# One-hot products for 36 groups of layer 1 and 20 of layer 0 in a two-layer GNN kernel

## The chip, the cores and the metric

The kernel runs on one core of one Trainium2 chip. The metric is the device time of one execution in microseconds. TensorE is called PE, VectorE DVE, ScalarE ACT, GpSimd POOL and SyncE SP.

## The reference

There are 12,500 nodes with 48 features and 200,000 edges, sorted by destination. Each layer reads, for every edge, the row of its source node, makes a message, and adds the messages up by destination.

```python
def _L0_gnn_ref(x, edge_index, edge_attr, W1, b1, W2, b2):
    src, dst = (edge_index[0], edge_index[1])
    tmp = jnp.concatenate([x[dst], x[src], edge_attr], axis=1)   # 48 + 48 + 32
    h = jax.nn.relu(tmp @ W1 + b1)                               # hidden 128
    msg = h @ W2 + b2                                            # 48
    return jax.ops.segment_sum(msg, dst, num_segments=N_NODES)

def _L1_gnn_ref(node_feat, edge_feat, src, dst, eps):
    m = jax.nn.relu(node_feat[src] + edge_feat)
    neigh = jax.ops.segment_sum(m, dst, num_segments=N_NODES)
    return (1.0 + eps[0]) * node_feat + neigh

x = _layernorm(x + _L0_gnn_ref(x, edge_index, edge_attr_32, W1, b1, W2, b2))
x = _layernorm(x + _L1_gnn_ref(x, edge_attr_48, src, dst, eps))
```

## The kernel before

The edges are padded to 391 groups of 512 (128 partitions x 4, `NCHUNK` = 391, `TPC` = 4). The nodes are 98 blocks of 128 (`NT` = 98), in 14 segments of 7 blocks (`NSEG`, `NB`). The two layers follow each other, since layer 1 gathers rows that layer 0's last segment writes.

The rows of the source nodes come by `gather` (L201): four indirect DMAs a group, issued by POOL, 128 rows each, from `x` in layer 0 (into the tile `cat`) and from `x1_dram` in layer 1 (into `xs`). The pool `cats` has ten buffers, so POOL can be ahead of the rest. SP loads the edge features for five groups at a time and, in layer 0, a window of projected destination rows (`wcat`) for every group.

The order on each engine is written out by hand. `run` (L443) goes over steps k; in each step it calls every stage for the group that is due, then `lead`. All engines work through their instructions in this order, so a stage's instructions stand behind those of the stages called ahead of it.

- Layer 0, step k: `fetch0` (gathers, five groups ahead), `fill0` (edge features and the one-hot of the destination, two ahead), `sum0` (group k-3: four matmuls of messages with the one-hots on L323, then a DVE addition into `agg` on L318), `message0` (k-2: matmuls on L432, bias on DVE), `hidden0` (k-1: matmul on L424, relu on ACT), `turn0` (k: four transposes on L417, copied by DVE to `cat_t`), then `lead0`, which loads and projects the next segment (`project`, 14 times: transposes L267, matmuls L272, with ACT copies between) at set steps.
- When the last group of a segment is summed, `finish0` transposes the sums, does residual and layer norm, writes `x1_dram`, and splits the result into three bfloat16 pieces that add up to it, in `xp` (128 x 98 blocks x 3 x 48, in SBUF).
- Layer 1, step k: `fetch1`, `fill1`, `sum1` (group k-1, matmuls and addition into `agg`), `message1` (k: DVE addition on L495, relu on ACT), then `lead1`.

For 28 of layer 1's groups (every 13th from 26) POOL gathers nothing. Their rows are made by products. `products` takes two such groups at a time. `place` turns their source indices into a tile `which` in PSUM that holds, for every edge, block + 1 at the row that the node has in its block, and zero elsewhere (DVE L515, PE transposes L520). For each of the 98 blocks `select` (L525) makes a one-hot of 128 x 1024 on DVE, and `multiply` (L530) does eight matmuls of 128 x 144 with the block's pieces in `xp`, added up in PSUM. At the end `edge_of` closes the sums, and three DVE reductions (L570) add the pieces up. The generator is advanced once a step, four blocks at a time (`BPS`). A batch of two groups takes 25 steps and one more for the end. PE multiplies in one step what DVE selected in the step before.

PSUM has eight banks. The sums of the products share the tiles `ph`, `pm` and `pt` with layer 0 (`pt` has two buffers), and `px` serves the projections and the ends of segments.

Of the kernel before, what the change touches and what calls it, by code (L numbers as in the profile page):

```python
# [58 lines left out]
FIRST = 26  # L59
EVERY = 13  # L60
NPE = 28
BATCH = 2
PIECES = 3
BPS = 4

PE_GROUPS = [FIRST + EVERY * i for i in range(NPE)]
assert PE_GROUPS[-1] < NCHUNK and NPE % BATCH == 0

# [60 lines left out]
def windowed(ctx, tc, dram, flag, x, src, dst, e32, e48, w1, b1, w2, b2, eps, out):  # L129
    nc = tc.nc  # L130
    const = ctx.enter_context(tc.tile_pool(name="const", bufs=1))
    onehots = ctx.enter_context(tc.tile_pool(name="onehots", bufs=2 * BPS))
# [90 lines left out]
    pb = psum.tile([P, NCHUNK], F32, name="px")  # L223
# [6 lines left out]
    def check_windows():  # L230
        flat = rel.rearrange("p g t -> p (g t)")
        most = node.tile([P, 1], F32, name="most")
        nc.vector.tensor_reduce(most, flat, AX.X, ALU.max)
        least = node.tile([P, 1], F32, name="least")
        nc.vector.tensor_reduce(least, flat, AX.X, ALU.min)
        over = node.tile([P, 1], F32, name="over")
        nc.vector.tensor_scalar(over, most, float(W), None, op0=ALU.is_ge)
        bad = node.tile([P, 1], F32, name="bad")
        nc.vector.scalar_tensor_tensor(bad, least, 0.0, over, op0=ALU.is_lt, op1=ALU.add)
        pf = psum.tile([1, 1], F32, name="px")  # L240
        nc.tensor.matmul(pf, bad, ones[:P, 0:1], start=True, stop=True)
        nc.vector.tensor_copy(flag, pf)


    part = const.tile([P, NPE, TPC], F32, name="part")
    block = const.tile([P, NPE, TPC], F32, name="block")

    def split_src():
        first = FIRST * TPC
        some = src_i[:, first : first + (NPE - 1) * EVERY * TPC].rearrange(  # L250
            "p (i c) -> p i c", c=EVERY * TPC
        )[:, :, 0:TPC]
        last = src_i[:, PE_GROUPS[-1] * TPC : (PE_GROUPS[-1] + 1) * TPC]
        bits = node.tile([P, NPE, TPC], I32, name="bits")
        for op, by, plus, to in (
            (ALU.bitwise_and, Q - 1, 0.0, part), (ALU.logical_shift_right, 7, 1.0, block)
        ):
            nc.vector.tensor_scalar(bits[:, : NPE - 1, :], some, by, None, op0=op)
            nc.vector.tensor_scalar(bits[:, NPE - 1, :], last, by, None, op0=op)
            nc.vector.tensor_scalar(to, bits, plus, None, op0=ALU.add)  # L260


    def project(s):
        for b, n in ((s * NB, 4), (s * NB + 4, 3)):
            pt = psum.tile([D, n, Q], F32, name="px")
            for k in range(n):
                nc.tensor.transpose(pt[:, k, :], x_seg[s][:, b + k - s * NB, :], ident)  # L267
            xt = node.tile([D, n, Q], F32, name="xt")
            nc.scalar.activation(xt, pt, AF.Copy)
            pa = psum.tile([Q, n, HID], F32, name="px")  # L270
            for k in range(n):
                nc.tensor.matmul(pa[:, k, :], xt[:, k, :], w1a, start=True, stop=True)  # L272
            a = node.tile([Q, n, HID], F32, name="a")
            nc.scalar.activation(a, pa, AF.Copy)
            row = b * Q - seg_start(s)
            nc.scalar.dma_start(
                a_dram[s][row : row + n * Q, :].rearrange("(t p) d -> p t d", p=Q), a
            )
            if b == s * NB and s > 0:
                row = b * Q - seg_start(s - 1)  # L280
                nc.scalar.dma_start(a_dram[s - 1][row : row + TAIL, :], a[0:TAIL, 0, :])
            if b > s * NB and s + 1 < NSEG:
                nc.scalar.dma_start(a_dram[s + 1][0:HEAD, :], a[Q - HEAD : Q, n - 1, :])
# [43 lines left out]
    def segment_sums(layer, s):  # L327
# [7 lines left out]
        pn = psum.tile([Q, NB, D], F32, name="px")  # L335
# [26 lines left out]
    def finish0(s):  # L362
# [6 lines left out]
        for i in range(PIECES):  # L369
            piece = xp[:, s * NB : (s + 1) * NB, i, :]  # L370
            nc.scalar.activation(piece, x1, AF.Copy)
            if i < PIECES - 1:
                rest = node.tile([Q, NB, D], F32, name="rest")
                nc.vector.tensor_tensor(rest, x1, piece, op=ALU.subtract)
                x1 = rest
# [20 lines left out]

    cat, ph, h, pm, hot = {}, {}, {}, {}, {}

    def fetch0(g):
        cat[g] = cats.tile([P, TPC, Q], F32, name="cat")  # L400
        for j in range(TPC):
            gather(cat[g][:, j, W : W + D], x, g, j)

    def fill0(g):
        e = load_edges("e32c", e32, DE, g)
        nc.scalar.activation(cat[g][:, :, W + D :], e, AF.Copy)
        one_hot(cat[g][:, :, :W], g)
# [6 lines left out]
    def turn0(g):  # L414
        pt = psum.tile([Q, TPC, P], F32, name="pt", bufs=2)
# [27 lines left out]
    def run(stages, finish, lead):  # L443
# [3 lines left out]
        for k in range(first, NCHUNK + last):  # L447
            for f, d in stages:
                g = k - d
                if 0 <= g < NCHUNK:  # L450
                    f(g)
                    if d == last:
                        for s in finishes.get(g, []):
                            finish(s)
            lead(k)

    def lead0(k):
# [7 lines left out]
        if k == 16:  # L465
            split_src()

    for g in range(AHEAD):
# [5 lines left out]
        finish0, lead0,  # L474
# [3 lines left out]
    made = {}  # L478

    def fetch1(g):  # L480
        if g in PE_GROUPS:
# [10 lines left out]
    def message1(g):  # L492
        m = work.tile([P, TPC, D], F32, name="m")
        xs = made.pop(g) if g in PE_GROUPS else cat.pop(g)
# [5 lines left out]
    def sum1(g):  # L500
        pa = reduce_tiles(hot.pop(g), h.pop(g))
        add_window(1, g, pa)


    tiles = BATCH * TPC
    PER = 512 // (PIECES * D)
    SUMS = ("ph", "pm", "pt")

    def place(first):

        which = psum.tile([Q, tiles, P], BF16, name="pt", bufs=2)
        for i in range(BATCH):
            which_e = work.tile([P, TPC, Q], BF16, name="which_e")
            for j in range(TPC):
                nc.vector.tensor_scalar(  # L515
                    which_e[:, j, :], iota_q, part[:, first + i, j : j + 1],
                    block[:, first + i, j : j + 1], op0=ALU.is_equal, op1=ALU.mult,
                )
            for j in range(TPC):
                nc.tensor.transpose(which[:, i * TPC + j, :], which_e[:, j, :], ident16)  # L520
        return which

    def select(which, b):
        o = onehots.tile([Q, tiles, P], BF16, name="o")
        nc.vector.tensor_scalar(o, which, float(b + 1), None, op0=ALU.is_equal)  # L525
        return o

    def multiply(ps, o, b):
        for k in range(tiles):
            nc.tensor.matmul(  # L530
                ps[k // PER][:, k % PER, :], o[:, k, :], xp[:, b, :, :],
                start=False, stop=False, skip_group_check=True,
            )

    def edge_of(ps, start):
        for t in ps:
            n = t.shape[1] * PIECES * D
            nc.tensor.matmul(
                t.rearrange("p k c d -> p (k c d)"), zeros[:, :P], zeros[:, :n],
                start=start, stop=not start,  # L540
            )

    zeros = const.tile([1, 512], BF16, name="zeros")
    nc.vector.memset(zeros, 0.0)

    def products():

        for first in range(0, NPE, BATCH):
            due = PE_GROUPS[first]
            which = place(first)  # L550
            ps = [
                psum.tile([P, min(PER, tiles - k * PER), PIECES, D], F32, name=name,
                          bufs=2 if name == "pt" else 1)
                for k, name in enumerate(SUMS)
            ]
            edge_of(ps, True)
            last = []
            for b in range(0, NT, BPS):
                now = [(b + i, select(which, b + i)) for i in range(min(BPS, NT - b))]
                for c, o in last:  # L560
                    multiply(ps, o, c)
                last = now
                yield due
            for c, o in last:
                multiply(ps, o, c)
            edge_of(ps, False)
            xs = work.tile([P, tiles, D], F32, name="made")
            for k, t in enumerate(ps):
                n = t.shape[1]
                nc.vector.tensor_reduce(  # L570
                    xs[:, k * PER : k * PER + n, :], t.rearrange("p k c d -> p k d c"),
                    AX.X, ALU.add,
                )
            for i in range(BATCH):
                made[PE_GROUPS[first + i]] = xs[:, i * TPC : (i + 1) * TPC, :]
            yield due

    work1 = products()

    def lead1(k):  # L580
        next(work1, None)
# [4 lines left out]
    run([(fetch1, -AHEAD), (fill1, -2), (sum1, 1), (message1, 0)], finish1, lead1)  # L586
# [211 lines left out]
```

## Time and profile before

| | |
|---|---|
| time, median of 10 runs | 3839.95 us (3836.3 to 3842.09) |
| the profiled execution | 3840.98 us, span 3839.2 us |
| mean granted PE clock | 0.786 of full |
| POOL, gathers of layer 0 | 1564, mean 949 ns, 1484.7 us busy |
| POOL, gathers of layer 1 | 1452, mean 962 ns, 1397.2 us busy |
| PE busy | 2849.9 us (74% of the span) |
| DVE busy | 1893.8 us (49%) |
| ACT busy | 564.0 us (15%) |

In a group's line the profile gives line, engine, operation, the tile written and those read, and the count; then busy time and mean duration of one; then the engine's idle time just before, with what ended it. In a timeline's line stand the start and the length in us, and in brackets the idle time ahead of it. The ends of matmuls are modelled, so starts are safer to compare than lengths. The line numbers are those of the kernel before.

### The profile page before, as it was taken

How to read it: one execution, taken by the hardware profiler on the slowest of the kernel's cores; microseconds unless marked ns; L12 is line 12 of the kernel's file. 1: busy time of each engine (PE TensorE's matmuls, PEld its weight loads, DVE VectorE, ACT ScalarE, POOL GpSimd, SP SyncE). 2: the span in 40 equal slices, each digit the busy share in tenths (PEclk: the TensorE clock that was granted, in tenths of full speed). 3: DMA queues.
4: the chain of work that ended last, by engine and by line, in shares of the span. 5: the costliest groups of instructions: out<-in, count | busy, mean ns of one | idle time of the engine just before them, and what ended most of it. 6: DMA issues, size and time to landing. Idle time of an engine off the chain costs nothing. (4 is left out here: it accounts for less than half of the span.)

```text
span 3839.2 us, 67581 instructions
## 1 busy us (share of the span) xinstructions
PE 2849.9 (74%) x23396; PEld 2202.8 (57%) x23396; DVE 1893.8 (49%) x4618; ACT 564.0 (15%) x1329; POOL 2883.8 (75%) x3025
## 2 busy tenths in 40 slices
PE   7888888888888888888876666667677676767631
PEld 4555555556555555556555666656666565656631
DVE  3333333333333333333356776767677677767731
ACT  2222212212212212212210000000000000000000
POOL 7777777777777777777767777777777777777776
PEclk8787777787777877877788888878877888888765
DMA  3222222222222222222222221222222222212221
GB/s 71 43 45 48 43 45 46 48 40 48 48 39 45 49 41 47 49 38 46 41 44 39 50 43 33 55 45 43 38 50 43 45 43 50 43 32 55 45 43 28
DMA packets 293005, 171.68 MB, mean 45 GB/s; under 512 B 109664, under 2 KB 292400, under 8 KB 292656
## 3 DMA queue, kind: packets, MB, share of 16 engines
q0 software_dynamic: 96512, 74.31, 14.4%
q1 hardware_dynamic: 179248, 84.31, 8.1%
q10 hardware_dynamic: 16896, 8.69, 0.8%
q8 instruction: 185, 3.03, 0.3%
q14 instruction: 164, 1.34, 0.1%
HBM read 154.45 MB, written 12.62 MB: 44 GB/s over the span
## 5 line engine op out<-in xcount | busy, mean ns | idle before, releaser
L201 POOL DMA_INDIRECT cat<-in_x_dram,src_i x1564 | 1484.7, 949 | 481.3 <-issue 343.5
L201 POOL DMA_INDIRECT xs<-x_dram,src_i x1452 | 1397.2, 962 | 458.4 <-issue 341.1
L530 PEld LDWEIGHTS <-o 128*128 128x128 bf16 x10976 | 849.1, 112 | 23.6 <-DVE o L525 1.0
L525 DVE TENSOR_SCALAR o<-pt 128x1024 bf16<-128x1024 bf16 x1372 | 848.6, 677 | 5.4 <-PE pt L520 5.4
L419 DVE COPY cat_t<-pt 128x512 f32<-128x512 f32 x391 | 270.1, 691 | 899.9 <-PE pt L417 899.9
L323 PE MATMUL pa<-hot,msg 128*48 128x48 f32 x3128 | 257.8, 235 | 557.4 <-ACT msg L497 557.1
L417 PEld LDWEIGHTS pt<-ident,cat 128*128 128x128 f32 x1564 | 264.1, 175 | 634.4 <-DMA cat<-in_x_dram,src_i 369.3
L424 PE MATMUL ph<-cat_t,wcat 128*128 128x512 f32 x782 | 573.7, 824 | 0.8 <-DVE cat_t L419 0.8
L323 PEld LDWEIGHTS pa<-hot,msg 128*48 128x48 f32 x3128 | 204.8, 145 | 640.9 <-ACT msg L497 620.9
L417 PE MATMUL pt<-ident,cat 128*128 128x128 f32 x1564 | 390.1, 348 | 242.7 <-DMA cat<-in_x_dram,src_i 238.7
L530 PE MATMUL ph<-xp,o 128*128 128x144 bf16 x4116 | 565.8, 255 | 0.2 <-DVE o L525 0.2
L530 PE MATMUL pm<-xp,o 128*128 128x144 bf16 x4116 | 563.8, 254 | 0.0
L432 PE MATMUL pm<-w_sb,h 128*128 128x48 f32 x3128 | 533.5, 324 | 1.3 <-ACT h L426 1.3
L432 PEld LDWEIGHTS pm<-w_sb,h 128*128 128x128 f32 x3128 | 480.0, 235 | 28.1 <-ACT h L426 2.3
L426 ACT ACTIVATE h<-ph,b_sb 128x512 f32<-128x512 f32 x391 | 268.4, 686 | 1363.4 <-PE ph L424 1345.5
L530 PE MATMUL pt<-xp,o 128*128 128x144 bf16 x2744 | 455.2, 254 | 0.0
L495 DVE TENSOR_TENSOR m<-xs,e48c 128x192 f32<-128x192 f32 x363 | 130.8, 360 | 541.4 <-DMA xs<-x_dram,src_i 540.4
L497 ACT ACTIVATE msg<-m 128x192 f32<-128x192 f32 x391 | 141.8, 363 | 1608.6 <-DVE m L495 1604.8
L323 PE MATMUL pa<-cat,msg 128*48 128x48 f32 x3128 | 263.0, 239 | 33.7 <-DVE msg L434 30.9
L323 PEld LDWEIGHTS pa<-cat,msg 128*48 128x48 f32 x3128 | 209.9, 148 | 113.0 <-issue 53.3
L434 DVE TENSOR_TENSOR msg<-pm,b_sb 128x192 f32<-128x192 f32 x391 | 139.3, 356 | 231.3 <-PE pm L432 230.6
L318 DVE TENSOR_TENSOR agg<-agg,pa 48x48 f32 x782 | 150.6, 193 | 175.3 <-PE pa L323 124.3
(79 smaller groups left out, 1063.5 us busy)
## 6 DMA issues: line engine op xcount, KB each, us to landing
e48c<-in_e_dram SPq DMA_DIRECT2D x78, 480.0 KB
cat<-in_x_dram,src_i POOLq DMA_INDIRECT x1564
e32c<-in_e_dram SPq DMA_DIRECT2D x78, 320.0 KB
xs<-x_dram,src_i POOLq DMA_INDIRECT x1452
wcat<-a SPq DMA_DIRECT2D x391, 24.0 KB
a<-a ACTq DMA_DIRECT2D x14, 256.0 KB
a<-a ACTq DMA_DIRECT2D x14, 192.0 KB
x_seg<-in_x_dram SPq DMA_DIRECT2D x14, 168.0 KB
```

The costliest lines, as they stand in the source:

```text
L201: nc.gpsimd.indirect_dma_start(out=t, out_offset=None, in_=table, in_offset=bass.IndirectOffsetOnAxis(ap=src_i[:, g * TPC + j : g * TPC + ...
L318: nc.vector.tensor_tensor(cols, cols, pa, op=ALU.add)
L323: nc.tensor.matmul(pa, msg[:, j, :], hot[:, j, :], start=j == 0, stop=j == TPC - 1)
L417: nc.tensor.transpose(pt[:, j, :], cat[g][:, j, :], ident[:P, :P])
L419: nc.vector.tensor_copy(cat_t, pt)
L424: nc.tensor.matmul(ph, wcats[g % NW], h[g], start=True, stop=True)
L426: nc.scalar.activation(t, ph, AF.Relu, bias=b1_sb)
L432: nc.tensor.matmul(pm[:, j, :], h[g][:, j, :], w2_sb, start=True, stop=True)
L434: nc.vector.tensor_tensor(msg, pm, b2_sb[:, None, :].to_broadcast([P, TPC, D]), op=ALU.add)
L497: nc.scalar.activation(msg, m, AF.Relu)
L525: nc.vector.tensor_scalar(o, which, float(b + 1), None, op0=ALU.is_equal)
L530: nc.tensor.matmul(ps[k // PER][:, k % PER, :], o[:, k, :], xp[:, b, :, :], start=False, stop=False, skip_group_check=True,)
```

## The change

- The groups by product are now given by `BY_PRODUCT`: ten pairs in layer 0 (first 54, next pair 33 on, the second group of a pair 16 after the first) at three blocks a step, and eighteen pairs in layer 1 (20, 20, 10) at five blocks a step. The gathers of these groups fall away: 80 in layer 0, and 32 more than before in layer 1.
- For layer 0 `xp` must hold the pieces of `x`. Whole segments of `x` are loaded in steps 2 to 15 and split two steps later. The pieces of layer 1's table then replace them: the segments that end before group 360 are loaded back from `x1_dram` and split from step 361 on, the last two are split in `finish0` as before.
- Layer 0's products are advanced at the end of `lead0` from step 18 on, so behind `turn0` and behind a projection. The finished rows are copied by ACT into `cat` in `fill0`.
- A batch ends and the next begins in the same call.
- In layer 1 the third one-hot of each step (`BY_ACT`) is written by ACT: Square of `which` minus block minus one, then Relu of one minus that.
- In layer 1 the addition into `agg` is a stage of its own (`add1`) at the end of the step, behind the products.
- PSUM: `which` and the three sums have banks of their own; `px` is gone, and projections, segment ends and `turn0` share `pt`, which has one buffer.

```diff
-FIRST = 26
-EVERY = 13
-NPE = 28
+BY_PRODUCT = ((54, 33, 16, 10, 3), (20, 20, 10, 18, 5))
+PE_GROUPS = [
+    [f + d * i + e * j for i in range(n) for j in range(2)] for f, d, e, n, _ in BY_PRODUCT
+]
 BATCH = 2
+BY_ACT = 2
 PIECES = 3
-BPS = 4
+SPLIT0 = 2
+BEGIN0 = 18
+END0 = 360
...
-    onehots = ctx.enter_context(tc.tile_pool(name="onehots", bufs=2 * BPS))
+    onehots = ctx.enter_context(tc.tile_pool(name="onehots", bufs=10))
...
+    def split(t, s):
+        for i in range(PIECES):
+            piece = xp[:, s * NB : (s + 1) * NB, i, :]
+            nc.scalar.activation(piece, t, AF.Copy)
+            if i < PIECES - 1:
+                rest = node.tile([Q, NB, D], F32, name="rest")
+                nc.vector.tensor_tensor(rest, t, piece, op=ALU.subtract)
+                t = rest
+    def load_whole(table, s):
+        whole[s] = node.tile([Q, NB, D], F32, name="whole")
+        nc.sync.dma_start(whole[s], rows_of(table, s))
...
     def project(s):
         for b, n in ((s * NB, 4), (s * NB + 4, 3)):
-            pt = psum.tile([D, n, Q], F32, name="px")
+            pt = psum.tile([D, n, Q], F32, name="pt")
...
+    def select(which, b, by_act):
+        o = onehots.tile([Q, which.shape[1], P], BF16, name="o")
+        if by_act:
+            square = work.tile([Q, which.shape[1], P], BF16, name="square", bufs=1)
+            nc.scalar.activation(square, which, AF.Square, bias=less[:, b : b + 1])
+            nc.scalar.activation(o, square, AF.Relu, bias=1.0, scale=-1.0)
+        else:
+            nc.vector.tensor_scalar(o, which, float(b + 1), None, op0=ALU.is_equal)
+        return o
...
     def fetch0(g):
         cat[g] = cats.tile([P, TPC, Q], F32, name="cat")
+        if g in PE_GROUPS[0]:
+            return
...
+        if g in PE_GROUPS[0]:
+            nc.scalar.activation(cat[g][:, :, W : W + D], made.pop((0, g)), AF.Copy)
...
     def turn0(g):
-        pt = psum.tile([Q, TPC, P], F32, name="pt", bufs=2)
+        pt = psum.tile([Q, TPC, P], F32, name="pt")
...
+        if k >= BEGIN0:
+            next(work0, None)
+        for s in range(NSEG):
+            if k == SPLIT0 + s:
+                load_whole(x, s)
+            if k == SPLIT0 + s + 2:
+                split(whole.pop(s), s)
+            if last_group(s) < END0:
+                if k == END0 + 2 * s + 1:
+                    load_whole(x1_dram, s)
+                if k == END0 + 2 * s + 4:
+                    split(whole.pop(s), s)
...
     def sum1(g):
-        pa = reduce_tiles(hot.pop(g), h.pop(g))
-        add_window(1, g, pa)
+        h[g] = reduce_tiles(hot.pop(g), h.pop(g))
+    def add1(g):
+        add_window(1, g, h.pop(g))
...
-    run([(fetch1, -AHEAD), (fill1, -2), (sum1, 1), (message1, 0)], finish1, lead1)
+    run(
+        [(fetch1, -AHEAD), (fill1, -2), (sum1, 1), (message1, 0),
+         (lambda g: next(work1, None), -AHEAD), (add1, 1)],
+        add1, finish1, lead1,
+    )
```

In `products` the `yield` behind the end of a batch is gone, and the tiles of the sums are named `sums0`, `sums1`, `sums2`.

## The prediction

> **What bounds the kernel now.** The page first: which engine is busy, and on what.
>
> ```profile
> PE 2849.9 (74%) x23396; PEld 2202.8 (57%) x23396; DVE 1893.8 (49%) x4618; ACT 564.0 (15%) x1329; POOL 2883.8 (75%) x3025
> ...
> L201 POOL DMA_INDIRECT cat<-in_x_dram,src_i x1564 | 1484.7, 949 | 481.3 <-issue 343.5
> L201 POOL DMA_INDIRECT xs<-x_dram,src_i x1452 | 1397.2, 962 | 458.4 <-issue 341.1
> ...
> L525 DVE TENSOR_SCALAR o<-pt 128x1024 bf16<-128x1024 bf16 x1372 | 848.6, 677 | 5.4 <-PE pt L520 5.4
> ```
>
> POOL is 75% "busy", but its idle time is 0.3 us of issue behind each gather. The timeline of POOL shows the only real hole:
>
> ```profile
> 1967.56 0.94 POOL L201 DMA_INDIRECT cat<-in_x_dram,src_i  x1 [0.31 <-issue]
> 1984.69 1.05 POOL L201 DMA_INDIRECT xs<-x_dram,src_i  x1 [16.19 <-issue]
> ```
>
> So layer 0's gathers run without a stop from 7.45 to 1968.50 us, 1.2539 us each, and layer 1's from 1984.69 to 3824.09 us, 1.2668 us each. A group of four takes 5.015 and 5.067 us. POOL sets the end in both layers.
>
> How near is TensorE? The timeline of PE around a projection in layer 0:
>
> ```profile
> 1038.18 0.60 PE L417 MATMUL pt<-ident,cat 128*128 128x128 f32 x4
> 1038.62 0.60 PE L267 MATMUL px<-ident,x_seg 128*48 128x128 f32 x4
> 1039.89 1.16 PE L272 MATMUL px<-w1a,xt 48*128 48x128 f32 x8 [0.68 <-ACT xt L269]
> 1041.74 0.51 PE L267 MATMUL px<-ident,x_seg 128*48 128x128 f32 x3 [0.69 <-ACT a L274]
> 1043.24 0.93 PE L272 MATMUL px<-w1a,xt 48*128 48x128 f32 x6 [0.99 <-ACT xt L269]
> 1044.10 0.87 PE L323 MATMUL pa<-cat,msg 128*48 128x48 f32 x8
> 1044.90 1.94 PE L432 MATMUL pm<-w_sb,h 128*128 128x48 f32 x8
> 1046.64 2.04 PE L424 MATMUL ph<-cat_t,wcat 128*128 128x512 f32 x2
> 1048.48 1.06 PE L417 MATMUL pt<-ident,cat 128*128 128x128 f32 x4
> 1049.47 0.88 PE L323 MATMUL pa<-cat,msg 128*48 128x48 f32 x8
> ```
>
> and, a little later, without the steps between:
>
> ```profile
> 1052.98 0.56 PE L323 MATMUL pa<-cat,msg 128*48 128x48 f32 x8
> ...
> 1055.85 0.56 PE L323 MATMUL pa<-cat,msg 128*48 128x48 f32 x8
> ```
>
> The windows put the clock beside them:
>
> ```profile
> 1044.50:1050.50 6.00, 6.00 (x29) 4.35 (x28) 1.48 (x4) 1.39 (x4) 4.48 (x6) 0.50 0.31 63
> 1051.00:1059.00 8.00, 8.00 (x62) 5.81 (x62) 3.72 (x11) 2.42 (x5) 5.87 (x8) 1.00 0.32 67
> 104.60:1762.00 1657.40, 1377.81 (x7593) 945.67 (x7593) 557.71 (x1463) 345.93 (x767) 1254.65 (x1322) 0.78 0.24 45
> ```
>
> (length, then busy PE, PEld, DVE, ACT, POOL, then granted clock.) A layer 0 step with PE never idle takes 2.87 us at clock 1.00 and 5.37 us at 0.50. The clock has only these two values, in stretches that are multiples of 3.4 us: in layer 0 it falls when a stretch's matmuls fill under about 0.65 of it, and comes back after one or two full ones. Layer 0's mean of 0.78 is thus a sign of slack, not a limit. The price of one product, in layer 1 (3, 3 and 2 matmuls a row):
>
> ```profile
> 2606.15 0.36 PE L530 MATMUL ph<-xp,o 128*128 128x144 bf16 x3
> ...
> 2608.03 0.29 PE L530 MATMUL pt<-xp,o 128*128 128x144 bf16 x2
> ```
>
> 30 matmuls start between these two: 62.7 ns each at full clock (120 ns at half).
>
> **POOL, layer 1.** Eight more groups skip their gathers: 32 x 1.2668 = 40.5 us. Can anything else be late there? Per 20-step batch POOL now needs 18 x 5.067 = 91.2 us. DVE: 20 x (m 0.36 + hot 0.34 + agg 0.19) = 18, 78 one-hots x 0.62 (their spacing) = 48, eight which_e and three sums 3.7, a share of the layer norms 4.6: 75 us. PE: a step is 40 x 62.7 ns + L323 0.49 + a turn 0.1 = 3.1 us, 62 a batch at full clock; at half 5.7 us, over POOL's 4.56, but the clock returned there within some 10 us of a batch change. ACT's two activations of 128x1024 are not in the trace: each lies between the 128x512 one (0.69 us, L426) and twice that; from the slope of 128x384 (0.49) to 128x512 (0.60) I take 1.04. With msg 0.36 that is 2.4 us a step, 3.1 at most, below 4.56. A batch change (5 us on PE and DVE) is covered by ten xs buffers, and groups by product take none. agg at the end of the step takes DVE's wait for PE from in front of m and the one-hots; DVE already sits waiting for xs (540.4 us), so I count nothing, and 0.2 us a step if that cover were gone. Layer 1: -40 us.
>
> **POOL, layer 0.** 80 gathers less: 80 x 1.2539 = 100.3 us, if POOL stays the end.
>
> **PE, layer 0.** Each of the 330 steps from k = 18 gets 24 matmuls behind turn0's transposes; everything PE does next waits for them. PE runs in order, so its sum decides. In full-clock time:
> - 330 steps x 2.87 = 947 us;
> - 7840 products x 62.7 ns = 492 us, and 0.04 us a step (0.14 into and 0.16 out of a burst against 0.26 without one) = 12;
> - ten changes of batch, now in one step: three stop matmuls 0.55, DVE's three sums 1.5 (0.60, 0.60, 0.45 on L570), eight which_e 2.2 with PE behind each, three start matmuls 0.55, hand-overs 0.4: 5.2 each = 52;
> - twelve projections: 5.5 (1038.62 to 1044.10), and 1.0 more since px is now pt and L267 must wait for cat_t's copy (0.69 us and two hand-overs): 78;
> - twelve finish0: L323 to the transposes 1.3, seven transposes 0.45, and 0.4 for msg behind the norm on DVE: 25.
>
> Sum 1606 us. POOL needs, for the same stretch, 312 groups x 5.015 = 1565. So PE becomes the bound even at full clock, by 41 us, and each stop makes the clock fall: after nine of the thirteen projections of layer 0 that follow the start it was 0.50 for 6.8 us (10 to 14 after the others), starting 4 to 6 us after the first L267, hence some 7 us beyond the projection, of which half is lost. 22 stops (projections, changes) x 3.5 = 77, and 8 for projections that run half in it: 1691 us. Group 18's transposes start at 103.4 us, so step 348 is at 1794. POOL then stands seven groups ahead (a cat buffer, one of ten, comes free in sum0, three steps behind turn0), and has 35 groups left to gather: 35 x 5.015 = 175.5. Last gather at 1970 us instead of 1968.5: the 100 us are gone.
>
> A rule that speaks against the change: the Trainium skill ("TensorE: Matmul & The Clock Gate", Back-to-back issue gap) gives a stream of weight loads and matmuls about 81 ns at 128 columns. The trace's 62.7 ns at 144 columns disagrees; at 81 ns an estimate from that page would add 18.3 ns x 7840 = 143 us.
>
> DVE in layer 0 adds 3 x 0.62 to about 1.6 us a step; with the norms that is 3.8 of PE's 4.5 to 5.1 us and a step ahead of PE: hidden. Do the one-hots disturb POOL? Between layer 0 (none) and layer 1 (four a step) the gather's cadence rises by 13 ns: 17 us over 1240 gathers, and nothing where POOL waits for buffers. The skill ("SBUF — State Buffer", Who interferes with whom) lets a DVE operation in a two-port mode lock GpSimd out for its whole length; an estimate by that rule and the 0.62 us row is 3 x 0.62 x 312 = 580 us, and layer 1's 13 ns show nothing of the kind for these.
>
> The splits: 14 loads of x in steps 2 to 15 and 12 of x1 in steps 361 to 383, 168 KB each on SP's queue ahead of wcat and e32c, three ACT copies (0.48) and two DVE subtractions (0.52) each; wcat is fetched three steps ahead. ACT is at 2 of 5 us there. Zero, and 14 x 1 us if a wcat came late; less in finish0 gains nothing, since the hole of 16.2 us ends with the write of x1. I leave the hole and the 16 us tail as they are.
>
> **Sum.** Profiled execution 3840.98 (span 3839.2, median of the runs 3839.95): +1.5 in layer 0, -40.5 in layer 1: 3802, which is 3801 beside the median.
>
> **Rivals.**
> - POOL stays the bound of both layers (PE's stops overlap, the clock stays up): -140.8, with 17 back if the cadence rises: 3699 to 3716, taken at 3708. For it: full-clock PE is only 41 us over, and POOL's lead of 35 us covers nearly that. Against: the stops are in the trace.
> - The clock costs more than I take: all 34 stops, finish0 included, end in a cold stretch of layer 0's mean length (8.8 us, 4.4 lost): 150 instead of 77, 3874, slower. Half-clock steps with products take 5.37 + 24 x 0.12 = 8.3 us. It decides from 39 us more than my sum, when some 250 of what are then 1730 us are at half clock, a granted clock of 0.93 in that stretch.
> - Layer 1 loses POOL as its bound: PE at half clock most of the time (1.1 us a step over POOL; a quarter of the steps is 110 us): 3910. Against it: busy PE brought the clock back every time.
>
> **Chances.** Forecast 0.50 (own range 3760 to 3845: 40 us either way for PE's sum), POOL 0.16, clock 0.28, layer 1 0.06. 0.2% is 7.7 us, about what a measurement here tells from no change. Of the forecast's 0.50, 0.41 is faster, 0.05 the same, 0.04 slower. Faster 0.41 + 0.16 = 0.57; same 0.06, with the edge of the clock case; slower 0.37. Range 3705 (most of the POOL case) to 3880 (the clock case, not the last).
>
> **What would show it.** Right: POOL idle before cat gathers for freed buffers (on PE's L351 or later) from about step 80, PE near 100% busy from 104 to 1790 us at a clock above 0.93, steps of 4.45 us there, last cat gather near 1970; layer 1 gathers still 1.27 us apart. Wrong: gathers 1.25 us apart all through layer 0 (the POOL case), a clock near 0.85 (the clock case), or xs gathers waiting.

## The result: slower by half a per cent, with layer 0 as forecast and layer 1 not

| | before | after |
|---|---|---|
| median time | 3840.15 us (28 runs) | 3860.25 us (8 runs, 3855.7 to 3864.63; two more, 3860.6 and 3876.9, are not among the eight) |
| ratio | | 1.0054, interval 1.0045 to 1.0063 |
| the profiled execution | 3840.98 us, span 3839.2 | 3860.6 us, span 3858.7 |
| mean granted PE clock | 0.786 | 0.908 |

The forecast was 3801 us, the range 3705 to 3880: the time lies inside, but the change was forecast as a gain of 39 us and is a loss of 20, on the side that the prediction gave 0.37. Several experiments below fell on chips where the kernel before itself took 4830 to 4915 us; of those runs the argument uses only what happens inside a step, and their totals decide nothing.

**Layer 0.** The timeline of POOL in the kernel after shows the hole between the layers, and one of the waits that were forecast:

```profile
1634.04 0.94 POOL L206 DMA_INDIRECT cat<-in_x_dram,src_i  x1 [11.80 <-issue]
...
1957.13 0.94 POOL L206 DMA_INDIRECT cat<-in_x_dram,src_i  x1 [0.31 <-issue]
1974.24 0.97 POOL L206 DMA_INDIRECT xs<-x_dram,src_i  x1 [16.17 <-issue]
```

The last cat gather ends at 1958.1 us, 10.4 us earlier than before, though 80 gathers (100 us) are gone. POOL waited 27 times, 97 us together, from step 102 on (forecast: from about 80). The profile names only "issue" for these waits, but 26 of the 27 end 0.77 us after PE has ended L351 for the tenth group before, the one whose `cat` buffer comes free; for the first line above that is

```profile
1632.68 0.59 PE L351 MATMUL pa<-cat,msg 128*48 128x48 f32 x8
```

The hole of 16 us is the same. The timeline of PE in the same layer, from one step to the next:

```profile
1001.46 0.56 PE L351 MATMUL pa<-cat,msg 128*48 128x48 f32 x8
...
1004.24 1.66 PE L453 MATMUL sums<-xp,o 128*128 128x144 bf16 x24
1005.83 0.56 PE L351 MATMUL pa<-cat,msg 128*48 128x48 f32 x8
```

From L351 to L351 it is 4.37 us with nothing idle: 2.87 and 24 products. The windows (columns as before: length, then busy PE, PEld, DVE, ACT, POOL, then granted clock), first from step 18 to step 348 of layer 0, then layer 1:

```profile
112.50:1781.60 1669.10, 1598.26 (x15558) 1312.06 (x15557) 1140.06 (x2539) 335.37 (x753) 1194.66 (x1264) 0.94 0.23 45
2000.00:3700.00 1700.00, 1214.80 (x16822) 1102.02 (x16820) 1194.72 (x2736) 893.82 (x1074) 1236.70 (x1287) 0.92 0.23 43
```

PE is 96% busy in the first, DVE 68%, at a clock of 0.94. In the second, PE is 71% busy, and no engine is full.

**Layer 1.** The xs gathers run from 1974.2 to 3843.6 us: 1869 us for 1420, where the kernel before took 1839 us for 1452 and the forecast was 1420 x 1.2668 = 1799. The waits view of the kernel after (engine, line, what it waited for: us in total, times, the longest):

```profile
DVE o L448 <- ACT square L445: 425.4, 342, 1.5
...
ACT square L445 <- DVE o L448: 413.1, 360, 8.4
```

The wait of DVE for Square comes in 342 of the 360 steps in which ACT writes a one-hot. The timeline of DVE and then of ACT, one step of layer 1 after:

```profile
2601.21 0.34 DVE L618 TENSOR_TENSOR m<-xs,e48c 128x192 f32<-128x192 f32 x1
2601.48 1.27 DVE L448 TENSOR_SCALAR o<-which 128x1024 bf16<-128x1024 bf16 x2
2603.99 1.29 DVE L448 TENSOR_SCALAR o<-which 128x1024 bf16<-128x1024 bf16 x2 [1.24 <-ACT square L445]
2605.20 0.18 DVE L346 TENSOR_TENSOR agg<-agg,pa 48x48 f32 x1
...
2605.58 0.34 DVE L618 TENSOR_TENSOR m<-xs,e48c 128x192 f32<-128x192 f32 x1
```

```profile
2601.65 0.36 ACT L620 ACTIVATE msg<-m 128x192 f32<-128x192 f32 x1 [0.96 <-DVE m L618]
2602.85 1.11 ACT L445 ACTIVATE square<-which,less 128x1024 bf16<-128x1024 bf16 x1 [0.84 <-DVE o L448]
2603.99 1.06 ACT L446 ACTIVATE o<-square 128x1024 bf16<-128x1024 bf16 x1
```

DVE writes one-hots 1 and 2. Only when the second ends does ACT's Square begin (2602.85), and only when Square ends does DVE write one-hots 4 and 5 (2603.99). The two engines read the same PSUM tile `which`, and the program holds a wait in each direction: Square waits for DVE's last reading of it, and DVE's next reading waits for Square. So Square does not run beside DVE's one-hots; it stands in their row, and only ACT's Relu and msg run beside them. From m to m the step is 4.37 us on DVE, of which 1.24 us is that wait. Twenty such steps and a change of batch are over POOL's 91.2 us: in the trace the batches begin 99 us apart (median of 17, by the first `which_e` of each). So DVE falls behind and the xs buffers come free late, 29 times by 0.7 to 8.6 us. The waits view of POOL in the kernel after has these 29 and two ordinary pauses of 0.3 us:

```profile
POOL xs L206 <- DVE m L618: 80.8, 31, 8.6
```

The account for layer 1: a gather takes 0.9616 us and 0.305 us to the next one, 1420 x 1.2666 = 1799 us, which is the forecast. The 29 waits are 80 us; 9 of these are the 0.305 that stand ahead of every gather, and the other 71 make it 1870, against 1869 seen. In the kernel before no xs gather waited longer than 0.6 us, the first one behind the hole left out. And DVE's own wait for gathers, 540.4 us before, fell to 75.8 us. What was cover for DVE is gone.

### The profile page after: what moved, and what is told of

The parts are those of the page before. It is cut to its first block, busy times and chain, and to the rows that moved or that the text cites. A ratio compares the mean times of both kernels' runs of the same rounds, so it can differ in the third digit from the quotient of the medians.

```text
span 3858.7 us, 93207 instructions
## 1 busy us (share of the span) xinstructions
PE 3117.6 (81%) x34568; PEld 2636.5 (68%) x34568; DVE 2538.0 (66%) x5826; ACT 1365.4 (35%) x2111; POOL 2776.8 (72%) x2914
## 5 line engine op out<-in xcount | busy, mean ns | idle before, releaser
L206 POOL DMA_INDIRECT cat<-in_x_dram,src_i x1484 | 1409.2, 950 | 546.1 <-issue 421.6
L448 DVE TENSOR_SCALAR o<-which 128x1024 bf16<-128x1024 bf16 x2384 | 1511.5, 679 | 435.8 <-ACT square L445 425.4
L453 PE MATMUL sums<-xp,o 128*128 128x144 bf16 x21952 | 1581.1, 234 | 5.6 <-ACT o L446 5.6
L453 PEld LDWEIGHTS <-o 128*128 128x128 bf16 x21952 | 1481.6, 102 | 35.0 <-ACT o L446 6.8
L351 PE MATMUL pa<-hot,msg 128*48 128x48 f32 x3128 | 230.4, 222 | 537.9 <-DVE agg L346 532.5
L351 PEld LDWEIGHTS pa<-hot,msg 128*48 128x48 f32 x3128 | 188.9, 135 | 603.1 <-ACT o L446 457.9
L445 ACT ACTIVATE square<-which,less 128x1024 bf16<-128x1024 bf16 x360 | 400.8, 1113 | 413.1 <-DVE o L448 413.1
L535 PE MATMUL ph<-cat_t,wcat 128*128 128x512 f32 x782 | 457.6, 669 | 0.8 <-DVE cat_t L530 0.8
L543 PE MATMUL pm<-w_sb,h 128*128 128x48 f32 x3128 | 450.0, 289 | 3.3 <-ACT h L537 3.3
L543 PEld LDWEIGHTS pm<-w_sb,h 128*128 128x128 f32 x3128 | 400.7, 201 | 26.1 <-ACT h L537 4.0
L446 ACT ACTIVATE o<-square 128x1024 bf16<-128x1024 bf16 x360 | 380.4, 1057 | 11.5
L528 PE MATMUL pt<-ident,cat 128*128 128x128 f32 x1564 | 258.4, 288 | 22.1 <-DMA cat<-in_x_dram,src_i 20.1
L351 PE MATMUL pa<-cat,msg 128*48 128x48 f32 x3128 | 227.3, 218 | 9.3 <-DVE msg L545 9.3
L351 PEld LDWEIGHTS pa<-cat,msg 128*48 128x48 f32 x3128 | 177.9, 129 | 66.1 <-issue 14.4
L618 DVE TENSOR_TENSOR m<-xs,e48c 128x192 f32<-128x192 f32 x355 | 122.2, 344 | 75.8 <-DMA xs<-x_dram,src_i 75.8
```

What stands on the lines that cost most here:

```text
L206: nc.gpsimd.indirect_dma_start(out=t, out_offset=None, in_=table, in_offset=bass.IndirectOffsetOnAxis(ap=src_i[:, g * TPC + j : g * TPC + ...
L351: nc.tensor.matmul(pa, msg[:, j, :], hot[:, j, :], start=j == 0, stop=j == TPC - 1)
L445: nc.scalar.activation(square, which, AF.Square, bias=less[:, b : b + 1])
L446: nc.scalar.activation(o, square, AF.Relu, bias=1.0, scale=-1.0)
L453: nc.tensor.matmul(ps[k // PER][:, k % PER, :], o[:, k, :], xp[:, b, :, :], start=False, stop=False, skip_group_check=True,)
L528: nc.tensor.transpose(pt[:, j, :], cat[g][:, j, :], ident[:P, :P])
```

## The experiments

**1. The wait itself: a copy of `which` for ACT.** The theory: the hand-over through one PSUM tile costs layer 1 its gain. Its rivals: the products on PE cost it; DVE's amount of work does, with or without the wait; or ACT and DVE slow each other when both are at work. (The recorded expectations give these theories letters, and not the same ones each time.) Once a batch, ACT copies `which` into SBUF (128 x 1024, bfloat16), and Square reads the copy. All else is as in the changed kernel.

```diff
+    def copy_for_act(which):
+        t = work.tile([Q, which.shape[1], P], BF16, name="which_s")
+        nc.scalar.activation(t, which, AF.Copy)
+        return t
...
-            nc.scalar.activation(square, which, AF.Square, bias=less[:, b : b + 1])
+            nc.scalar.activation(square, own, AF.Square, bias=less[:, b : b + 1])
```

> The changed kernel, but ACT copies the tile which to SBUF once a batch (layer 1) and Square reads that copy: the same work on DVE, one activation a batch more on ACT, and no tile in PSUM that both read, so that the two no longer stand in each other's order. Theory A (the hand-over between DVE and ACT over which is what costs): a DVE step goes from 4.37 us to 4 x 0.62 + 0.65 = 3.1 us, and DVE's wait for Square (1.24 us in each step, 425 us in all) is gone; where POOL bounds layer 1 that is 1800 us and a kernel of 3790. Theory B (ACT and DVE at work at the same time slow each other, or ACT's activations are too long): the step stays near 4.4 us. In the condition of the last runs (kernel before at 4840 us) the changed kernel's 1.0935 goes to about 1.08, as with dve_only; read the steps.

Measured: 3819.58 us (4 runs, 3816.97 to 3822.45) beside 3847.47 of the kernel before, ratio 0.9922 (0.9906 to 0.9939). The step on DVE in the timeline of this kernel:

```profile
3000.45 0.34 DVE L624 TENSOR_TENSOR m<-xs,e48c 128x192 f32<-128x192 f32 x1
3000.72 2.47 DVE L453 TENSOR_SCALAR o<-which 128x1024 bf16<-128x1024 bf16 x4
...
3003.50 0.34 DVE L624 TENSOR_TENSOR m<-xs,e48c 128x192 f32<-128x192 f32 x1
```

The four one-hots follow each other, and the step is 3.05 us (3.1 expected). The number of one-hots on DVE, of products on PE and of gathers is the same as in the changed kernel, and ACT and DVE now do work at the same time, so the rivals fall, and the wait is shown to be the cause of the late buffers. No xs gather waits any more, and DVE waits for gathers again, as its waits view says:

```profile
DVE m L624 <- DMA xs<-x_dram,src_i: 487.6, 226, 4.9
```

So POOL bounds layer 1 again, as the prediction had it, but not at its price, and the 3790 us that were expected are missed by 30. The gathers of layer 1 on the page of this kernel:

```profile
L206 POOL DMA_INDIRECT xs<-x_dram,src_i x1420 | 1400.9, 987 | 452.4 <-issue 353.3
```

A gather takes 987 ns instead of the 962 of the kernel before (on its page in the prediction). With 0.305 us between them they take 1834 us, 1.2913 each, instead of the 1799 forecast. What the longer ones have beside them is in the last section.

**2. Is it PE? Half of the products of layer 1 left out.** The matmuls of every odd block are left out in layer 1, so this kernel doesn't add up all rows there.

```diff
-                    multiply(ps, o, c)
+                    if layer != 1 or c % 2 == 0:
+                        multiply(ps, o, c)
```

The first run of it:

> In layer 1 the matmuls of the odd blocks are left out; the one-hots are still made, by DVE and ACT as in the changed kernel. Theory A (hand-over between DVE and ACT): layer 1 stays at 1860 to 1868 us, the kernel at 3850 to 3860, steps of 4.37 us on DVE. Theory C (PE, with the addition into agg now behind the products): PE has 2.5 us less a step every other block, layer 1 goes to 1800, the kernel to 3790.

and the second:

> The same kernel as half_l1 (in layer 1 the matmuls of the odd blocks are left out, the one-hots are still made by DVE and ACT). Theory A (the hand-over between DVE and ACT): layer 1 stays at 1860 to 1868 us and DVE's step at 4.37 us, the kernel at 3850 to 3860. Theory C (PE): layer 1 goes to 1800, the kernel to 3790.

Measured: 5025.58 us beside 4837.57 of the kernel before, and 5040.47 beside 4843.92. The totals say nothing. The timeline of DVE inside a step does (second run):

```profile
3005.34 0.20 DVE L346 TENSOR_TENSOR agg<-agg,pa 48x48 f32 x1
...
3008.51 1.29 DVE L448 TENSOR_SCALAR o<-which 128x1024 bf16<-128x1024 bf16 x2 [1.24 <-ACT square L445]
3009.72 0.19 DVE L346 TENSOR_TENSOR agg<-agg,pa 48x48 f32 x1
```

With half of PE's products gone the step is 4.38 us and the wait 1.24 us, as in the changed kernel itself, which was run in the same condition too:

> The changed kernel itself, to learn whether the first eight runs (where the kernel before took 4840 us, and kernels with more instructions lost more) say anything of the case's own condition. If time there goes by the number of instructions (67,581 before, 93,207 after; 1000 us / 67,581 = 14.8 ns more for each), this kernel takes 3860 + 93,207 x 14.8 ns = 5240 us where the kernel before takes 4840; if the kernel before is back at 3840, this one is at 3860 again.

It took 5364.45 us beside 4911.87 (5240 was expected). The commonest distance from one `hot` to the next was 4.37 us (about 160 of 390); PE's stops, told of in the last section, lengthen many of the others.

**3. DVE writes all five one-hots.** The other way to take the wait away: ACT's share goes back to DVE.

```diff
-BY_ACT = 2
+BY_ACT = -1
```

Three runs of it:

> All five one-hots of a layer 1 step on DVE, none on ACT; the rest as in the changed kernel. Theory A (what makes layer 1 slow is that DVE's fourth one-hot waits for ACT's Square, which waits for DVE's second, so that a DVE step is 4.37 us): without the hand-over a DVE step is 5 x 0.62 + 0.65 = 3.75 us, 84 us a batch with the batch change and the norms, under POOL's 91.2. The xs gathers run at 1.27 us again without waiting for buffers, layer 1 takes 1420 x 1.267 = 1799 us instead of 1868, the kernel 3790. Theory B (DVE's mere amount of work, five selects or the shorter batches): DVE does more work, so layer 1 is slower than 1868 us, the kernel over 3870. Theory C (PE bounds layer 1): no change, 3860.

> The same kernel as dve_only (all five one-hots of a layer 1 step on DVE), again, since in the first call the kernel before itself took 4838 us. Theory A (DVE's fourth one-hot waits for ACT's Square, which waits for DVE's second: a DVE step of 4.37 us): without the hand-over a DVE step is 5 x 0.62 + 0.65 = 3.75 us; layer 1 is bound by POOL, 1420 x 1.267 = 1799 us instead of 1868; the kernel 3790, 1.3% under the kernel before. Theory B (DVE's amount of work): layer 1 over 1868 us, the kernel over 3870. Theory C (PE bounds layer 1): 3860.

> All five one-hots of a step in layer 1 are written by VectorE, none by ScalarE. If the hand-over between the two engines is what cost layer 1 its gain: VectorE's step falls from 4.37 to about 3.65 us (five selections and 0.65 us), 20 steps and what lies between them fit under POOL's batch of about 91 us, the stalls of the xs gathers vanish, and the time is 3790 us if those gathers keep 1.27 us each, 3825 if they take 1.29 as in own_copy. If the loss is TensorE's: the time stays at 3860.

Measured, in this order: 5241.44 us beside 4837.57 (ratio 1.0839), 5240.13 beside 4843.92 (1.0819), and 5328.39 beside 4913.6, ratio 1.0845 (1.0795 to 1.0895). The totals cannot tell whether it beats the kernel before where that takes 3840 us. Its commonest step is 3.64 us in all three (3.65 and 3.75 were expected): 0.73 us less than the changed kernel's, though DVE writes a one-hot more. Timeline of DVE in the second of them:

```profile
3009.68 3.07 DVE L448 TENSOR_SCALAR o<-which 128x1024 bf16<-128x1024 bf16 x5
3012.68 0.19 DVE L346 TENSOR_TENSOR agg<-agg,pa 48x48 f32 x1
```

Five one-hots take 3.00 us to the next instruction; the changed kernel's four with Square between them take 3.72 (2601.48 to 2605.20). As written, ACT's help costs DVE 0.72 us a step.

**4. ACT writes the last one-hot of the step, not the third.** If the two take turns at the tile, ACT's turn beside agg, hot and m should cost less than one in the middle.

```diff
-BY_ACT = 2
+BY_ACT = 4
```

Two runs of it:

> ACT writes the fifth one-hot of a layer 1 step instead of the third: the same work on every engine. Theory A: Square still waits for DVE's fourth one-hot, but what DVE does next (agg, hot, m: 0.65 us) needs no ACT, so that only about 0.6 of the 1.24 us is left as a wait: a DVE step of about 3.8 us, layer 1 bound by POOL, 1800 to 1815 us, the kernel 3790 to 3805. Theories B and C: the work is the same, 3860.

> The same kernel as act_last (ACT writes the fifth one-hot instead of the third). Theory A: agg, hot and m (0.65 us of DVE) now lie beside Square, so that about 0.6 of the 1.24 us is left as a wait: a DVE step of about 3.8 us, layer 1 bound by POOL, 1800 to 1815 us, the kernel 3790 to 3805. Theories B and C: 3860.

Measured: 5231.82 us beside 4837.57 (ratio 1.0853), and 5240.95 beside 4843.92 (1.082, 1.0769 to 1.0871). In the timeline of DVE in the second the wait stands ahead of the step's first one-hot and is half as long:

```profile
3004.99 2.48 DVE L448 TENSOR_SCALAR o<-which 128x1024 bf16<-128x1024 bf16 x4 [0.60 <-ACT square L445]
```

This is the turn-taking again: Square's 1.11 us and the two hand-overs, less the 0.65 us of the three instructions that don't read `which`. The total stays open.

**5. Layer 0: fewer products, and experiment 1's copy.** Does PE bound layer 0 of the changed kernel, or POOL? Fewer groups by product are less work for PE and more gathers, so the two theories differ in sign. 14 groups instead of 20, spread over the same stretch, with the copy of experiment 1 in layer 1:

```diff
-BY_PRODUCT = ((54, 33, 16, 10, 3), (20, 20, 10, 18, 5))
+BY_PRODUCT = ((70, 49, 24, 7, 2), (20, 20, 10, 18, 5))
```

> The kernel of own_two4 once more, for its total in the condition in which the kernel before takes 3840 us. If TensorE bounds layer 0 with 20 groups by products, 14 groups leave POOL as the bound there: last cat gather near 1898 us, 53 earlier than in own_copy, and a time near 3767 us. If POOL is the bound already with 20 groups, the 24 gathers more cost 30 us: near 3850.

Measured: 3770.54 us (4 runs, 3766.15 to 3772.62) beside 3841.49 of the kernel before, ratio 0.9814 (0.9798 to 0.9831). It beats both kernels, and experiment 1 as well. The timeline of POOL at the end of its layer 0, and the cat gathers on its page:

```profile
1911.57 0.95 POOL L206 DMA_INDIRECT cat<-in_x_dram,src_i  x1 [0.31 <-issue]
1928.53 0.94 POOL L206 DMA_INDIRECT xs<-x_dram,src_i  x1 [16.02 <-issue]
```

```profile
L206 POOL DMA_INDIRECT cat<-in_x_dram,src_i x1508 | 1446.0, 959 | 463.8 <-issue 338.4
```

24 gathers more than in experiment 1, and the last cat gather ends at 1912.5 us instead of 1951.4. So the products, and not POOL, are shown to bound layer 0 with 20 groups; that it is PE's part of them and not DVE's, experiment 6 shows. With 14 the waits of POOL for cat buffers (23 in experiment 1, 85 us together) are all gone, and POOL sets the pace: 1508 gathers from 7.1 to 1912.5 us are 1.2635 us each. Expected were 1.254 and a last gather near 1898; the 9.5 ns more on each are the 14 us between. The time itself was expected at 3767.

The same kernel in three earlier runs gave 5223.94 beside 4913.6 (ratio 1.0628), 5136.93 beside 4848.29 (1.0606, 1.0588 to 1.0624) and 5217.03 beside 4911.15 (1.0619); 14 groups with DVE writing all one-hots gave 5161.65 beside 4829.94 (1.0682, 1.0629 to 1.0735; about 5100 was expected):

> own_copy with 14 groups by products in layer 0 instead of 20, spread over the same stretch, so 6 groups more are gathered (24 gathers). If TensorE bounds layer 0 with 20 groups, 14 leave POOL as the bound: 1508 gathers at 1.254 us, last cat gather near 1898 us, 53 earlier than in own_copy, and a time near 3767 us. If POOL is the bound already with 20 groups, the 24 gathers cost 30 us: near 3850.

> The same kernel as own_two3, for its total in the condition in which the kernel before takes 3840 us. If TensorE bounds layer 0 with 20 groups by products, 14 groups leave POOL as the bound there: last cat gather near 1898 us, 53 earlier than in own_copy, and a time near 3767 us. If POOL is the bound already with 20 groups, the 24 gathers more cost 30 us: near 3850.

> The kernel of own_two4 once more, for its total in the condition in which the kernel before takes 3840 us. If TensorE bounds layer 0 with 20 groups by products, 14 groups leave POOL as the bound there: last cat gather near 1898 us, 53 earlier than in own_copy, and a time near 3767 us. If POOL is the bound already with 20 groups, the 24 gathers more cost 30 us: near 3850.

> Two edits of the changed kernel: all one-hots of layer 1 on DVE, and in layer 0 seven pairs of groups at two blocks a step (14 groups) instead of ten pairs at three. Theory: in layer 0 PE has 2.87 + 16 x 0.063 = 3.9 us of a step, with its stops 4.5, under POOL's 4.8, so POOL bounds it: 1508 gathers, last one at 7.5 + 1508 x 1.254 = 1898 us; layer 1 by POOL too, 1799 us: 1898 + 16 + 1799 + 16 = 3730, 3% under a kernel before of 3840. The rival, that the products' steps cost what they cost in the changed kernel whatever their number, gives 3850. Where the kernel before takes 4840 (time by the number of instructions), its 87,000 or so instructions give about 5100, 5% over.

So a change that gains 1.9% on one chip loses 6% on another.

**6. Layer 0's part, more ways.** The changed kernel without every odd block's matmuls in layer 0 (so not all rows are added up there), and layer 0's part of the change alone:

```diff
-                    multiply(ps, o, c)
+                    if layer != 0 or c % 2 == 0:
+                        multiply(ps, o, c)
```

> In layer 0 the matmuls of the odd blocks are left out (half of the products' matmuls; the one-hots are still made). Theory: PE bounds layer 0 in steps 18 to 348. 3920 x 62.7 ns = 246 us less for PE, which then has slack, so that POOL bounds again: last gather of layer 0 at 7.5 + 1484 x 1.254 = 1868 us instead of 1958, the kernel about 3770. If DVE's or ACT's added work or the wcat loads bound layer 0, the last gather stays near 1958 and the kernel at 3860.

> The same kernel as half_l0 (in layer 0 the matmuls of the odd blocks are left out). Theory: PE bounds layer 0 in steps 18 to 348; with 246 us less for PE the last gather of layer 0 ends near 1868 us instead of 1958 and the kernel takes about 3770. If DVE, ACT or the wcat loads bound layer 0, 1958 and 3860 stay.

> The changed kernel with the matmuls of every odd block left out in layer 0's products; all else is as in the changed kernel. If TensorE bounds layer 0: POOL takes over, 1484 gathers at 1.254 us, last cat gather near 1868 us, time near 3770. If it does not: last gather stays at 1958 and the time at 3860.

```diff
-BY_PRODUCT = ((54, 33, 16, 10, 3), (20, 20, 10, 18, 5))
+BY_PRODUCT = ((54, 33, 16, 10, 3), (26, 26, 13, 14, 4))
-BY_ACT = 2
+BY_ACT = -1
```

> Layer 0 as changed (20 groups by products); layer 1 as in the kernel before (28 groups, four blocks to a step, none written by ScalarE), but with the sums added at the end of a step. If the two layers' parts are separate: last cat gather at 1958 us, layer 1 as before at 1839 us after the 16 us between them, together 3830 us, 10 below the kernel before. If the change of layer 0 costs layer 1 something (its products end later, the split of the nodes' values in the middle), the time is 3840 or more.

The first gave 5153.28 beside 4837.57, 5120.89 beside 4843.92 and 5208.35 beside 4913.6 in its three runs, and the second 5155.41 beside 4913.6, ratio 1.0478 (1.043 to 1.0526). In this condition PE also stops where the profile shows nothing that it waits for (last section), so neither total stands for or against PE as the bound. The steps of the first kernel do. DVE writes the same three one-hots in each, but PE now has 8 products in one step and 16 in the next. The timeline of PE in its third run:

```profile
1255.15 0.56 PE L351 MATMUL pa<-cat,msg 128*48 128x48 f32 x8
...
1257.93 0.66 PE L453 MATMUL sums<-xp,o 128*128 128x144 bf16 x8
1258.53 0.56 PE L351 MATMUL pa<-cat,msg 128*48 128x48 f32 x8
...
1261.31 1.16 PE L453 MATMUL sums<-xp,o 128*128 128x144 bf16 x16
1262.40 0.56 PE L351 MATMUL pa<-cat,msg 128*48 128x48 f32 x8
```

The steps are 3.38 and 3.87 us, 2.87 and 8 or 16 x 62.7 ns, where the changed kernel takes 4.37 with 24. These two lengths are the commonest in all three runs. So the step goes by PE's products, with DVE's work left as it was. What layer 0's part gives alone is thus read from the trace of the changed kernel (10 us), and not measured as a total.

## Why the prediction was wrong

- **Layer 0, PE's sum: right, with some luck.** Forecast 1691 us from step 18 to step 348, seen 1669 (112.5 to 1781.6). The product at 62.7 ns was seen at 62.7, the typical step forecast at 4.45 us was 4.37, the clock above 0.93 was 0.94. But 198 us of that stretch were at half clock, so some 99 lost, against 85 forecast for it (in the kernel before it was ten of the thirteen projections that had 6.8 us at half clock behind them, not nine, which moves the sum little); what is left, 1570 us, is 36 less than the 1606 forecast at full clock. By this estimate PE at full clock would have been over POOL's 1565 by some 5 us, not 41, and the rest of what it was over came with the clock. The start was 9 us later than counted (112.5 for 103.4). These errors partly cancel: the last gather, forecast for 1970, ended at 1958. The trace has the 62.7 ns of the row, not the 81 ns at 128 columns of the Trainium skill ("TensorE: Matmul & The Clock Gate", Back-to-back issue gap); an estimate with the 81 would have put the end of that stretch some 140 us later.
- **The two rivals of layer 0** (POOL stays the bound, the clock costs 73 us more) did not come. POOL's 97 us of waits and experiments 5 and 6 speak against the first, the clock of 0.94 against the second.
- **The hole and the tail: right**, 16.2 us and 15.2.
- **Layer 1, the size of ACT's work: right.** Square 1.11 us and Relu 1.06, for 1.04 each. ACT's load of a step was taken at 2.4 us and was 2.5.
- **Layer 1, DVE's 75 us a batch: the step that failed.** The prediction added up DVE's and ACT's durations apart and compared each with POOL's 91.2 us. It left out that both read one PSUM tile, and that the program then makes each wait for the other: 1.24 us in 342 of 360 steps, 425 us in all, 24 us a batch. 75 and 24 are 99, as seen, and more than POOL's 91.2. So xs gathers waited, one of the signs that the prediction had named for being wrong, and layer 1 took 1869 us for 1799. With layer 0's 12 us less, that is the whole way from 3802 to 3860. Experiment 1 takes that wait away, and layer 1's gathers end 1834 us after their start: half of the 70 us that were missed.
- **The other half, hidden behind the first: POOL's price.** The gathers were taken at 1.2668 us; with the wait gone they take 1.2913, 35 us in all (experiment 1; 1.2853 in experiment 5). So without the hand-over layer 1 would have gained some 6 us on the kernel before (1833.6 for 1839.4), not 40. The prediction had such a term (17 us, "if the cadence rises"), but in the other layer and in a rival. In the changed kernel itself it plays no part: its gathers take 0.962 us, and only the waits are new.
- **The rival "layer 1 loses POOL as its bound"** had the right place and a chance of 0.06, but laid it to PE's clock. The clock in layer 1 was 0.92, higher than before (0.81), and with half of PE's products left out the step stayed as it was (experiment 2). That the time lies inside the range is luck too: the part of it above 3845 was there for the clock's case in layer 0.
- **agg behind the products**: counted at nothing, 0.2 us a step if DVE's cover were gone. The cover did go, through the hand-over. What agg cost then was not measured by itself. In experiment 1, where agg stands as in the changed kernel, it takes no time from a gather.

## What to carry to other kernels

When part of one engine's work is given to another, look at what both read, and for the waits that the program puts between them. Here a tile in PSUM that two engines read by turns made one row of their work: the helper's 1.11 us and the hand-overs were added to the busy engine's time, more than the 0.62 us of a one-hot that were taken from it. Give the helper a copy, and set the sum of a whole step, waits included, against what the bound engine allows. Where two engines are close to being the bound, less of the work moved can be worth more: with 14 groups layer 0's gathers ended 39 us earlier than with 20.

## What the runs showed of the hardware

- **Gathers beside short SBUF operations.** In layer 1 most gathers take 0.945 us and a few over 1.05: 163 of 1420 in the kernel with ACT's copy (experiment 1), 120 of 1452 before, 71 of 1420 after. What lies over 0.945 us adds up to 59 us of xs gathers in that kernel, 25 before and 24 after. Between 2000 and 3700 us `hot` or `m` (0.34 us each, float32 operations of DVE whose inputs and output are in SBUF) runs beside 97% of the long ones in experiment 1, 97% before and 88% after, and beside 39%, 45% and 31% of those under 1.0 us. One-hots, which read PSUM, run beside 69% to 89% of the short ones, so one of them alone doesn't lengthen a gather. It matters when `hot` starts: in experiment 1, where it starts within 0.1 us of the start of a gather, 114 of 121 gathers are long (mean 1.31 us); where it starts 0.1 to 0.9 us later, none of 200. Before it is 69 of 72 and none of 262. After, only 16 gathers start so, 7 of them long, and 9 of the 262 others are. By this reading the gathers of experiment 1 cost more because more of them start together with `hot`; no run here shifts `hot` to try it.
- **A chip on which instructions cost more.** On four of the chips the kernel before took 4830 to 4915 us, 990 to 1075 more, and on one of these the changed kernel took 1500 more. Divided by the instructions of the program (67,581 and 93,207) it is 14.6 to 15.9 ns each before and 16.1 after. PE's instructions alone (46,792 and 69,136) fit as well, with 21 to 23 ns and 22; the runs don't tell the two apart. In the changed kernel there PE stops some 1300 times behind "issue", 1000 us together, mostly in bunches of half a dozen within some 6 us; where it took 3860 us PE stops so once. Why, no run here shows. The change adds 38% to the instructions, and is 9.4% slower there (ratio 1.0935, 1.091 to 1.096).
